# The last pass of an edge convolution: the halves of a row sum added on POOL, and one row product for each quad where there were two

## The chip, the cores and the metric

The kernel runs on one NeuronCore of a Trainium2 chip. The metric is the device time of a run in microseconds. The engines are named as in the profile: PE (TensorE, matrix products), PEld (its weight loads), DVE (VectorE), ACT (ScalarE), POOL (GpSimd) and SP (SyncE, which here only issues transfers). Each engine works through its own instructions in a fixed order and waits on semaphores where an operand comes from another engine.

## The reference

A graph with 6,250 nodes of 128 features and 200,000 edges, sorted by destination, passes through two networks: five attention layers, and then one edge convolution. The change lies in the convolution:

```python
x_src, x_dst = h[src], h[dst]
e = (x_dst - x_src) @ theta_w.T + x_src @ phi_w.T
e = relu(bn(e, bn0_g, bn0_b))      # batch norm over all edges
e = e @ fc1_w.T
e = relu(bn(e, bn1_g, bn1_b))      # batch norm over all edges
agg = segment_sum(e, dst, num_segments=n)
x = agg / maximum(cnt, 1)[:, None]
out = x0 + relu(x + h)             # h is the layer-normed x0, x0 the input plus the attention's output
```

The two batch norms need the mean and the variance over all edges before the next step can be done, so the convolution takes three passes over the edges. The last one computes the second activation and sums the edges of each destination.

## The kernel before

**Rows and quads.** The edges of a destination are put into slots of four (K = 4), padded where they don't fill the last slot. 128 slots, one on each partition, make a *quad* of 512 edges. QM = 412 quads are always worked on; more exist only for inputs that need them, under a branch on a count (`over`), and are not run here. In the convolution a *block* is GQ = 4 quads, G = 16 columns of 128 edges, so each of the three passes has 103 blocks.

**The three passes.** The first (lines 941 to 967) gathers the two nodes' terms of each edge with indirect transfers that POOL issues, and writes the pre-activations `e0_d` to DRAM. The second (1005 to 1014) reads them back, applies the first batch norm and ReLU and takes the statistics of the product with fc1. The third (1061 to 1089), the one that is changed, reads `e0_d` again and does this for each block `i`:

- SP issues the loads of `es` (1 MB, line 1065, three buffers) and of `neq` (line 1067, three buffers), a mask that says which slots belong to which destination.
- ACT applies the first batch norm and ReLU to `es` (1068), and makes the selection matrix `oh` = 1 - `neq` in float32 (1070, two buffers).
- For each quad PE multiplies four columns of 128 edges by `fs`, the scaled fc1 weights (1075), into one PSUM tile `rps` of four buffers, and DVE adds the shift `shr` on the way into `rt` (1076, two buffers).
- ACT applies the ReLU to the whole of `rt` (1077). `rt` is now, for each of four quads, four rows of 128 features on each partition, one for each edge of the slot.
- DVE adds the first two of the four to the last two (1079), giving `r2` (two buffers), with two rows per slot.
- PE adds up slots of one destination: `oh` times each of the two rows, accumulated in PSUM in `po` (1083; the profile calls it `pos`). That is two products for each quad, eight in a block.
- DVE makes the running state (1086): `state` x `keep` + `po`. `keep` is 0 where a new window of destinations begins. Each of the four updates needs the one before it. `st` has three buffers of four states.
- POOL copies each state to its place in `A2`, a table in SBUF (1089). The place is read from a register, and a later quad of the same window overwrites an earlier one.

**What sets the order.** No order is written out by hand. Tiles and their buffers are declared, and a scheduler in the framework orders the instructions of each engine when the program is built, from its own estimate of the durations, and puts in the semaphore waits. Work of neighbouring blocks is thus interleaved: in the timeline the state updates of one block stand between the additions 1076 of the next. On the chip each engine keeps that order.

After the last block, DVE and POOL combine the even and odd windows of `A2` (1096 to 1098), and DVE does the closing arithmetic (1106 to 1114).

Of the kernel before, what the change touches and what calls it, by code (L numbers as in the profile page):

```python
# [9 lines left out]
F32 = mybir.dt.float32  # L10
# [3 lines left out]
OP = mybir.AluOpType  # L14
# [7 lines left out]
P = 128  # L22
K = 4
G = 16
GQ = G // K
# [9 lines left out]
def gnn_kernel(ctx: ExitStack, tc: tile.TileContext, x, src, dst, ea, Ws, Wes, a_srcs, a_dsts, a_edges,  # L35
# [13 lines left out]
    nc = tc.nc  # L49
# [84 lines left out]
    def regs(row, q0, n, engine, top):  # L134
        _, r = nc.values_load_multi_w_load_instructions(
            tbi[32 * row:32 * row + 1, ds(q0, n)], engines=[engine], min_val=0, max_val=top, skip_runtime_bounds_check_because="blocks' views are below W2")
        return r

    def over(step, do, before=None, between=None):

        for q0 in range(0, QM, step):
            do(q0, min(step, QM - q0))
        if QM < Q:
            if between:
                between()
            n = nc.values_load_multi_w_load_instructions(more, min_val=0, max_val=P * Q, skip_runtime_bounds_check_because="a count of rows")[1][0]
            with tc.If(n > 0):
                if before:
                    before()
                for q0 in range(QM, Q, step):  # L150
                    do(q0, min(step, Q - q0))

    def mid_bc(a, n, w):
        return a[:, None, :].to_broadcast([P, n, w])

    def last_bc(a, n, w):
        return a[:, :, None].to_broadcast([P, n, w])
# [25 lines left out]
    with tc.tile_pool(name="gat", bufs=1) as gp:  # L183
# [305 lines left out]
        def rows(sp, sw, pp, then):  # L489
# [83 lines left out]
            def with_then(q0, n):  # L573
                some(q0, n)
                if q0 == 4 * RQ:
                    then()
# [203 lines left out]
        def edges(l):  # L780
            with tc.tile_pool(name="edg", bufs=2) as ep, tc.tile_pool(name="edgp", bufs=1, space=PSUM) as pp:
# [92 lines left out]
                def fixed():  # L874
                    nc.vector.tensor_copy(was, state[0])
                    state[0] = was

                over(AQ, some, lambda: nc.scalar.dma_start(ael[:, K * QM:], ae_d[l, :, K * QM:]), fixed)

        with tc.tile_pool(name="row", bufs=1) as sp, tc.tile_pool(name="roww", bufs=3) as sw, \  # L880
# [19 lines left out]
    with tc.tile_pool(name="ec", bufs=1) as gp:  # L900
# [10 lines left out]
        with tc.tile_pool(name="p1", bufs=2) as ep, tc.tile_pool(name="p1p", bufs=4, space=PSUM) as pp:  # L911
# [29 lines left out]
            def some(q0, n):  # L941
# [25 lines left out]
                nc.sync.dma_start(e0_d[c0 // G], xs.rearrange("p a b -> p (a b)"))  # L967

            over(GQ, some)

        nc.vector.tensor_reduce(S1, st0[:, 0, :], AX.X, OP.add)
# [81 lines left out]
        with tc.tile_pool(name="p4", bufs=3) as ep, tc.tile_pool(name="p4p", bufs=4, space=PSUM) as pp:  # L1053
            A2 = ep.tile([P, W2, D], F32, name="A2", bufs=1)
            A2f = A2.rearrange("p b d -> p (b d)")
            nc.gpsimd.memset(A2, 0.0)
            was = ep.tile([P, D], F32, name="was4", bufs=1)
            nc.vector.memset(was, 0.0)
            state = [was]

            def some(q0, n):
                i = q0 // GQ
                r = regs(2, q0, GQ, POOL, (W2 - 2) * P)
                es = ep.tile([P, G, P], F32, name="e4")
                nc.sync.dma_start(es.rearrange("p a b -> p (a b)"), e0_d[i])
                neq = ep.tile([P, GQ, P], BF, name="neq4")
                nc.sync.dma_start(neq, neq_d[i])
                nc.scalar.activation(es, es, AF.Relu, bias=SH0, scale=SC0)
                oh = ep.tile([P, GQ, P], F32, name="oh4", bufs=2)
                nc.scalar.activation(oh, neq, AF.Identity, bias=onec, scale=-1.0)  # L1070
                rt = ep.tile([P, GQ, K, P], F32, name="rt", bufs=2)
                for q in range(GQ):
                    ps = pp.tile([P, K, P], F32, name="rps")
                    for k in range(K):
                        nc.tensor.matmul(ps[:, k, :], es[:, K * q + k, :], fs, start=True, stop=True)
                    nc.vector.tensor_tensor(rt[:, q], ps, mid_bc(shr, K, P), OP.add)
                nc.scalar.activation(rt, rt, AF.Relu)
                r2 = ep.tile([P, GQ, K // 2, P], F32, name="r2", bufs=2)
                nc.vector.tensor_tensor(r2, rt[:, :, :K // 2, :], rt[:, :, K // 2:, :], OP.add)
                po = pp.tile([P, GQ, P], F32, name="pos")  # L1080
                for q in range(GQ):
                    for k in range(K // 2):
                        nc.tensor.matmul(po[:, q, :], oh[:, q, :], r2[:, q, k, :], start=(k == 0), stop=(k == K // 2 - 1))
                st = ep.tile([P, GQ, P], F32, name="st4")
                for q in range(GQ):
                    nc.vector.scalar_tensor_tensor(st[:, q, :], state[0], keep[:, q0 + q:q0 + q + 1], po[:, q, :], op0=OP.mult, op1=OP.add)  # L1086
                    state[0] = st[:, q, :]
                for q in range(GQ):
                    nc.gpsimd.tensor_copy(A2f[:, ds(r[q], 2 * P)].rearrange("p (a d) -> p a d", a=2), mid_bc(st[:, q, :], 2, P))  # L1089

            def fixed():
                nc.vector.tensor_copy(was, state[0])
                state[0] = was

            over(GQ, some, between=fixed)
            nc.vector.tensor_tensor(A, A2[:, 0:2 * NB:2], last_bc(mX, NB, D), OP.mult)
            nc.gpsimd.tensor_tensor(A2[:, 1:2 * NB:2], A2[:, 1:2 * NB:2], last_bc(mY, NB, D), OP.mult)
            nc.vector.tensor_tensor(A, A, A2[:, 1:2 * NB:2], OP.add)  # L1098
# [60 lines left out]
```

## Time and profile before

| | us |
|---|---|
| median of 3 runs | 17,761.48 (17,751.63 to 17,762.48) |
| profiled execution | 15,354.99 |
| its span, first to last instruction | 15,353.2 |
| last pass within it | 14,707 to 15,280 |
| closing arithmetic | 15,280 to 15,353 |

The profiled execution is one run of the same program with the hardware profiler on. It is 2,406 us shorter than the median of the runs without it; nothing in the profile says where. Times of instructions and waits come from this execution.

In the profile, `r<-rt` is the addition at 1079, with the buffer numbers left out (`r2`), `pos` is the PSUM tile `po`, `e` is the tile `es`, and `A` is `A2` in this stage. One float32 product shows as two records of 128 columns on PE, so the eight products of line 1083 in a block are 16 records. A bracket at the end of a line of a timeline is the idle time before it, with what ended it; "issue" means that the profile shows no releaser. A merged line with "x2" gives the time from the first start to the last end. Consecutive instructions of an engine overlap by some tens of nanoseconds, so distances between starts are shorter than durations.

### The profile page before, as it was taken

What the parts mean: (1) busy time and instruction counts of PE and PEld (TensorE: products, weight loads), DVE (VectorE), ACT (ScalarE), POOL (GpSimd) and SP (SyncE); (2) the same over time, 40 slices, a digit from 0 to 9 for tenths busy, and PEclk for the clock granted to TensorE, in tenths of its full rate; (3) what the DMA queues carried; (4) which work ended last, traced back from release to release, by engine and by line L of the source; (5) the groups of instructions that cost most, each with busy time, mean ns of one, the idle gap of its engine ahead of it and who ended that gap; (6) DMA issues with size and microseconds to landing.
All of it is one profiled execution on the core that took longest, in us unless ns stands there. A gap on an engine that the chain in (4) does not pass through costs nothing. (4 is left out here: it accounts for less than half of the span.)

```text
span 15353.2 us, 84839 instructions
## 1 busy us (share of the span) xinstructions
PE 3563.2 (23%) x18550; PEld 2269.4 (15%) x18550; DVE 9106.1 (59%) x14785; ACT 3161.7 (21%) x6154; POOL 10194.1 (66%) x10906
## 2 busy tenths in 40 slices
PE   5211111121111121111121111211111232222797
PEld 4100000010000010000010000100000111111377
DVE  8535666656666656666656666656666643333688
ACT  1221111111111111111111111111111211111476
POOL 1667777747777747777657777477777477777134
PEclk7555555555555555555555555555555555555899
DMA  3212222222222222222222222222222333333665
GB/s 123 61 50 71 67 67 67 66 64 67 66 67 67 64 62 67 67 67 67 60 66 67 67 67 67 57 70 67 67 67 66 91 117 111 111 113 112 230 231 192
DMA packets 722984, 1301.20 MB, mean 85 GB/s; under 512 B 207200, under 2 KB 503552, under 8 KB 682624
## 3 DMA queue, kind: packets, MB, share of 16 engines
q0 software_dynamic: 329600, 663.87, 17.7%
q1 hardware_dynamic: 356416, 587.30, 11.5%
q10 hardware_dynamic: 36416, 44.22, 0.9%
q8 instruction: 159, 2.61, 0.1%
q14 instruction: 393, 3.22, 0.1%
HBM read 1094.17 MB, written 200.45 MB: 84 GB/s over the span
## 5 line engine op out<-in xcount | busy, mean ns | idle before, releaser
L791 POOL DMA_INDIRECT g<-table,srci x8240 | 7780.3, 944 | 2565.9 <-issue 2490.9
L810 PE MATMUL xp<-ident,z 128*128 128x128 f32 x2060 | 507.2, 427 | 7548.2 <-DVE z L807 7548.2
L804 DVE TENSOR_TENSOR mt<-g,ael 128x32 f32<-128x32 f32 (+1 forms) x260 | 57.1, 219 | 3563.2 <-DMA g<-table,srci 3532.1
L945 POOL DMA_INDIRECT g<-btable,srci x1648 | 1573.0, 954 | 502.7 <-issue 478.8
L854 DVE TENSOR_REDUCE ys<-pr 128x1032 f32<-128x4128 f32 (+1 forms) x260 | 1841.4, 7082 | 8.8
L810 PEld LDWEIGHTS xp<-ident,z 128*128 128x128 f32 x2060 | 403.6, 223 | 7728.6 <-DVE z L807 7326.7
L866 PE MATMUL op<-y,oh 128*128 128x387 bf16 x2060 | 840.2, 511 | 1528.5 <-DVE ys L867 848.1
L850 DVE TENSOR_TENSOR pr<-g,mt 128x4128 f32<-128x4128 f32 (+1 forms) x260 | 1147.2, 4412 | 70.5 <-ACT mt L847 70.5
L872 ACT COPY sv<-st 128x260 f32 x2060 | 834.6, 405 | 1272.5 <-DVE u L821 1118.4
L867 DVE TENSOR_REDUCE ys<-op 128x258 f32<-128x774 f32 x1030 | 998.8, 970 | 105.7 <-PE op L866 81.9
L858 ACT CAST y<-ys 128x1032 bf16<-128x1032 f32 (+1 forms) x260 | 265.1, 1020 | 3825.7 <-DVE ys L857 3825.7
L960 DVE TENSOR_TENSOR xe<-g,ar 128x512 f32<-128x512 f32 x412 | 282.0, 687 | 1115.5 <-DMA g<-btable,srci 1115.3
L856 ACT CAST y<-ys 128x1032 bf16<-128x1032 f32 (+1 forms) x260 | 264.5, 1017 | 2816.7 <-DVE ys L854 2816.7
L516 POOL DMA_INDIRECT rg<-rec_d,rowi x412 | 468.1, 1136 | 419.6 <-ACT neqw L533 273.6
L963 PE MATMUL xps<-ident,xe 128*128 128x128 f32 x1648 | 441.7, 424 | 1239.4 <-DVE xe L960 1239.4
L869 DVE SCALAR_TENSOR_TENSOR st<-st,cor,ys 128x129 f32<-128x129 f32 x2055 | 710.6, 346 | 9.4
L966 ACT ACTIVATE sq<-xps,negc 128x512 f32<-128x512 f32 x412 | 281.6, 686 | 1699.1 <-DVE xs L964 1698.4
L963 PEld LDWEIGHTS xps<-ident,xe 128*128 128x128 f32 x1648 | 294.2, 216 | 1418.3 <-issue 1405.0
L866 PEld LDWEIGHTS <-oh 128*128 128x128 bf16 x2060 | 200.0, 119 | 1937.7 <-issue 850.3
L813 DVE TENSOR_REDUCE tm<-xp 128x8 f32<-128x1024 f32 (+1 forms) x260 | 315.7, 1214 | 238.2 <-PE xp L810 238.2
L1089 POOL COPY A<-st 128x256 f32 x412 | 248.5, 603 | 313.2 <-DVE st L1086 297.2
L861 ACT ACTIVATE oh<-neq,onesq 128x1024 bf16<-128x1024 bf16 (+1 forms) x260 | 296.1, 1139 | 475.3 <-PE op L866 428.7
(389 smaller groups left out, 9385.0 us busy)
## 6 DMA issues: line engine op xcount, KB each, us to landing
g<-table,srci POOLq DMA_INDIRECT x8240, 2.5
e_d<-xs SPq DMA_DIRECT2D x103, 1024.0 KB, 4.3
x<-e_d SPq DMA_DIRECT2D x103, 1024.0 KB, 4.8
e<-e_d SPq DMA_DIRECT2D x103, 1024.0 KB, 4.9
neq<-neq_d SPq DMA_DIRECT2D x255, 256.0 KB, 3.1
eqt<-eqt_d SPq DMA_DIRECT2D x255, 256.0 KB, 2.7
g<-btable,srci POOLq DMA_INDIRECT x1648, 2.5
table<-hb SPq DMA_DIRECT2D x80, 195.0 KB, 2.5
```

The source lines that it names most:

```text
L516: nc.gpsimd.indirect_dma_start(out=rg[:, j, :, :].rearrange("p k r -> p (k r)"), out_offset=None, in_=rec_d, in_offset=bass.IndirectOffset ...
L791: nc.gpsimd.indirect_dma_start(out=g[:, j, :], out_offset=None, in_=table, in_offset=bass.IndirectOffsetOnAxis(ap=srci[:, c0 + j:c0 + j + ...
L810: nc.tensor.transpose(xp[:, j, :], z[:, j, :], ident)
L813: nc.vector.tensor_reduce(tm[:, :n], xp[:, :n], AX.X, OP.max)
L850: nc.vector.tensor_tensor(pr.rearrange("p q k d -> p (q k) d")[:, :w], g[:, :w, :D + 1], last_bc(ex, w, D + 1), OP.mult)
L854: nc.vector.tensor_reduce(y, pr[:, :n].rearrange("p q k d -> p q d k"), AX.X, OP.add)
L866: nc.tensor.matmul(op[:, j, :3 * (D + 1)], oh[:, h + j, :], y3[:, h + j], start=True, stop=True)
L867: nc.vector.tensor_reduce(sm, op[:, :, :3 * (D + 1)].rearrange("p b (a d) -> p b d a", a=3), AX.X, OP.add)
L869: nc.vector.scalar_tensor_tensor(st[:, j, :D + 1], state[0][:, :D + 1], cor[:, j:j + 1], sm[:, j - h, :], op0=OP.mult, op1=OP.add)
L872: nc.scalar.copy(svf[:, ds(r[j], 2 * HW)].rearrange("p (a w) -> p a w", a=2), mid_bc(st[:, j, :], 2, HW))
L945: nc.gpsimd.indirect_dma_start(out=g[:, j, :], out_offset=None, in_=btable, in_offset=bass.IndirectOffsetOnAxis(ap=srci[:, c0 + j:c0 + j + ...
L963: nc.tensor.transpose(ps[:, k, :], xe[:, k, :], ident)
```

## The change

POOL adds the two rows of `r2` to one row `r1`, and PE multiplies `oh` with that one row. A block has one POOL instruction of 128 x 512 elements more and four row products instead of eight. All else stays as written: the loads, the ACT instructions, the additions and updates on DVE, and the copies on POOL. `r1` has two buffers of 2 KB on each partition.

```diff
                 r2 = ep.tile([P, GQ, K // 2, P], F32, name="r2", bufs=2)
                 nc.vector.tensor_tensor(r2, rt[:, :, :K // 2, :], rt[:, :, K // 2:, :], OP.add)
+                r1 = ep.tile([P, GQ, P], F32, name="r1", bufs=2)
+                nc.gpsimd.tensor_tensor(r1, r2[:, :, 0, :], r2[:, :, 1, :], OP.add)
                 po = pp.tile([P, GQ, P], F32, name="pos")
                 for q in range(GQ):
-                    for k in range(K // 2):
-                        nc.tensor.matmul(po[:, q, :], oh[:, q, :], r2[:, q, k, :], start=(k == 0), stop=(k == K // 2 - 1))
+                    nc.tensor.matmul(po[:, q, :], oh[:, q, :], r1[:, q, :], start=True, stop=True)
                 st = ep.tile([P, GQ, P], F32, name="st4")
```

## The prediction

> **What bounds the kernel now.** I read the stretches of the profiled span first, to find the stage that the diff touches. The last pass runs from 14,707 to 15,280 us of the 15,353.2 us span. The groups by shape give the durations, the waits in the steady part of the stage say what each engine lacks, and the timeline of each engine shows the order. The chain that ended last is of no use: it covers only the closing vector work after this stage.
>
> Columns: length, busy time and count of each engine, then PE clock, DMA share and GB/s.
> ```profile
> core 0: us, PE busy (x) PEld busy (x) DVE busy (x) ACT busy (x) POOL busy (x), PEclk, DMA share, GB/s
> 14720.00:15270.00 550.00, 548.61 (x4896) 547.40 (x4895) 483.98 (x916) 464.26 (x303) 244.16 (x404) 1.00 0.63 216
> ```
> PE has no idle time in this stage and has its full clock, so it sets the pace; DVE is busy 88%, ACT 84%, POOL 44%. The first state update begins at 14,729.1 us and the last at 15,278.6 us, 411 updates apart and four to a block: 549.5/411 x 4 = 5.348 us a block, for 103 blocks. Each engine's share of that is PE 5.35, DVE 483.98/550 x 5.348 = 4.71, ACT 4.51 us.
>
> Groups of instructions by shape (count | total, mean ns | idle before, releaser):
> ```profile
> L1075 PE MATMUL rps<-fs,e 128*128 128x128 f32 x3296 | 387.7, 276 | 4.4 <-DMA e<-e_d 4.4
> L1076 DVE TENSOR_TENSOR rt<-rps,shr 128x512 f32<-128x512 f32 x412 | 269.1, 682 | 14.5 <-PE rps L1075 9.4
> L1089 POOL COPY A<-st 128x256 f32 x412 | 248.5, 603 | 313.2 <-DVE st L1086 297.2 <-POOL A L1089 0.2
> L1083 PE MATMUL pos<-r,oh 128*128 128x128 f32 x1648 | 203.2, 277 | 4.2 <-DVE r L1079 4.2
> L1077 ACT ACTIVATE rt<-rt 128x2048 f32<-128x2048 f32 x103 | 196.7, 1909 | 30.4 <-DVE rt L1076 29.3
> L1086 DVE SCALAR_TENSOR_TENSOR st<-st,keep,pos 128x128 f32<-128x128 f32 x411 | 140.4, 342 | 62.2 <-issue 53.8 <-PE pos L1083 6.3
> L1079 DVE TENSOR_TENSOR r<-rt 128x1024 f32<-128x1024 f32 x103 | 125.4, 1217 | 1.7 <-ACT rt L1077 1.7
> ```
> A block holds 32 records of L1075 and 16 of L1083 (each float32 product is two records). Their 276 ns overlap; the pace is 5.348/48 = 111 ns.
>
> Two blocks on DVE, and what PE and POOL do meanwhile (start, duration, engine, line):
> ```profile
> 15004.19 1.22 DVE L1079 TENSOR_TENSOR r<-rt 128x1024 f32<-128x1024 f32 x1
> 15005.33 0.34 DVE L1086 SCALAR_TENSOR_TENSOR st<-st,keep,pos 128x128 f32<-128x128 f32 x1
> 15005.58 1.28 DVE L1076 TENSOR_TENSOR rt<-rps,shr 128x512 f32<-128x512 f32 x2
> 15007.63 0.35 DVE L1086 SCALAR_TENSOR_TENSOR st<-st,keep,pos 128x128 f32<-128x128 f32 x1 [0.77 <-issue]
> ...
> 15009.61 1.22 DVE L1079 TENSOR_TENSOR r<-rt 128x1024 f32<-128x1024 f32 x1
> 15010.74 0.34 DVE L1086 SCALAR_TENSOR_TENSOR st<-st,keep,pos 128x128 f32<-128x128 f32 x1
> 15011.00 1.88 DVE L1076 TENSOR_TENSOR rt<-rps,shr 128x512 f32<-128x512 f32 x3
> 15013.21 0.73 DVE L1086 SCALAR_TENSOR_TENSOR st<-st,keep,pos 128x128 f32<-128x128 f32 x2 [0.34 <-issue]
> ```
> ```profile
> 15005.58 1.95 PE L1083 MATMUL pos<-r,oh 128*128 128x128 f32 x16
> ```
> ```profile
> 15004.41 1.80 POOL L1089 COPY A<-st 128x256 f32 x2 [0.57 <-DVE st L1086]
> 15008.11 0.40 POOL L1089 COPY A<-st 128x256 f32 x1 [1.91 <-DVE st L1086]
> ```
> The reader is to see a ring. r2 ends at 15,005.41; the row product starts 0.17 later and holds PE for 1.79 us; the first state update follows 0.26 after it. That is 2.22 us from r2's end to the update. DVE fills it with the previous block's last update (0.26) and two or three additions L1076 (0.60 each: three take 1.88, of which one is 0.68), then waits 0.77 or 0.34 us. The order on each engine was fixed when the program was built, and it isn't the order of the source.
>
> **What the Trainium skill says.** "SBUF — State Buffer", section "Who interferes with whom": a DVE instruction with two SBUF inputs and a GpSimd instruction that reads SBUF lock each other out for a whole instruction. The trace agrees: a copy L1089 takes 403 ns by its median, but the two at 15,004.41 take 1.80 us; the first had to wait for r2, the one DVE operation here with two SBUF inputs. "GPSIMD Engine Reference", section 3.1, has a float32 add of 2048 elements at 4497 ns; in proportion my estimate for 512 is 1.12 us. The trace has the same shape of addition in an earlier stage, and it also shows the lock from the other side (DVE 1.69 us where 0.68 is usual):
> ```profile
> 12110.33 1.26 POOL L709 TENSOR_TENSOR xb<-xb,bb 128x512 f32<-128x512 f32 x1 [13.09 <-DVE x1c L632]
> 12110.45 1.69 DVE L716 TENSOR_TENSOR h2c<-x1c,m 128x512 f32<-128x512 f32 x1
> ```
> I take 1.26 us for the new addition; the bounds are 1.12 (the page) and 2.25 (1.26 and a full r2 in front).
>
> **The change part by part.**
> *Removed:* 8 of the 48 PE records of a block, 8 x 0.111 = 0.89 us. PE falls to 4.46 us, under DVE's 4.71. PE's whole 0.89 x 103 = 92 us can't be gained, because DVE takes over at 4.71: at most (5.348 - 4.71) x 103 = 66 us.
> *Added:* 103 additions on POOL of 1.26 us. POOL then has 2.37 (now) + 1.26 = 3.6 us of work a block, so it isn't the bound. Queued behind the addition on POOL are the copies L1089; nobody waits for those inside the stage except the state tile's third buffer, three blocks later. Its cover lost, a late copy costs nothing until it is that late. No DMA is added or moved, and SP's queue is unchanged. ACT and DVE keep their instructions. r2's buffer comes free at POOL's read instead of PE's, earlier or equal. oh is freed by the row product, which is later by the new step; oh's next write on ACT comes at 15,008.77, 1.2 us after the product ended, which just covers that.
> *Lengthened:* the ring. From r2's end: the copy that r2 locked out runs first (0.40, and 0.05), addition 1.26, hand-over to PE 0.17, product 0.89, hand-over to DVE 0.26: 3.03 us. If no copy is in front: 0.13 (the hand-over from an update to a copy, 15,004.28 to 15,004.41) + 1.26 + 0.17 + 1.15 = 2.71. So 2.71 to 3.03 against 2.22 now.
> *What hides it:* additions L1076 that DVE can do before the update. PE, not held by the row product, goes on with the next block's products while POOL adds, and PSUM holds four of them, so four additions can be there. With the update of 0.26 in front these are 0.26 + 4 x 0.60 = 2.66 us: DVE waits 0.05 to 0.37, mean 0.21. The other waits of DVE in this stretch were for products and for ACT, 6.6 us, 0.06 a block. Sum: 4.71 + 0.21 + 0.06 = 4.98 us a block. DVE is the bound then, so every further wait costs its full length. If the cover is gone altogether, with two additions as at 15,005.58, the wait is 1.25 to 1.57.
>
> Gain: (5.348 - 4.98) x 103 = 38 us. The profiled execution's 15,354.99 us (span 15,353.2 and 1.8 us around it) would be about 15,317. The median of the runs shown is 17,761.48, which is 2,406 us above the profiled one; the profile can't show where. I take this stage to be the same in both and subtract there: 17,723. If everything were stretched alike (1.157), it would be 44 us.
>
> **The rivals.** They differ in how many additions the fixed order leaves between r2 and the first update.
> *A, four:* as above, -38 us (own range -65, no waiting, to -20). For it: PE is free for 1.6 us more before the row product. 48 in 100.
> *A', more than DVE's limit:* if PE's clock without the profiler is below the 1.00 shown, PE stays the bound and all of its saving counts: at 0.9 of the clock 0.89/0.9 x 103 = -102 us. Nothing speaks for it but the 2,406 us. 6 in 100.
> *B, three or a mixture of three and four:* work 2.06 to 2.36, waits 0.35 to 0.97, period 5.12 to 5.74; the means of the two ends give -7 us for the mixture and +24 for three. The removed PE time has turned into DVE waits. 20 in 100, 4 of them beyond the bound.
> *C, slower, the order stays as it is:* two and three in turn, mean work 1.76, waits 0.95 to 1.27, period 5.72 to 6.04: +38 to +71, mean +55 us, 17,816. It decides from a wait of 0.92 us a block on, where the period passes 5.69. For it: DVE's additions there are now just those that were ready before the row product, and the order's maker may price the POOL step too low and the lock not at all. Against it: that maker placed PE's products with no idle time now. 26 in 100.
> *DMA takes over:* 1 MB a block lands in 4.9 us, share 0.63; at 4.98 us the share is 0.68, and the stage before this one ran at 0.83 (14,500 to 14,600 us). Excluded as the bound.
>
> **How the numbers follow.** 0.2% is 35.5 us, about what a measurement of this kernel tells from no change. Faster beyond it: 42 of A's 48 and A', 48 in 100. Within: 6 of A and 16 of B, 22. Slower: C and 4 of B, 30. Time of the likeliest: 17,723, its own range 17,696 to 17,741. The range over the cases, A to most of C: 17,690 to 17,822.
>
> **What would show it.** Right: L1083 with 824 records, PE at about 0.9 busy in this stage, DVE at 0.94 or more, the POOL addition at 1.2 to 1.8 us, four L1076 between r2 and the first update, and its wait under 0.4 us. C: two or three there and waits near 1 us, PE with idle time before L1083 put down to POOL. Wrong in size: a DVE r2 longer than 1.22 (locked out by POOL), an addition behind several copies, ACT waiting at L1070 for the product, or a PE clock under 1.00 in the gaps.

## The result, and the profile after

| | before | after |
|---|---|---|
| median, us | 17,755.09 | 17,816.7 |
| runs | 7 (17,751.63 to 17,770.11) | 7 (17,803.64 to 17,824.07) |
| ratio, 95% interval | | 1.0033 [1.0023, 1.0042] |
| last pass, first to last state update, us | 549.5 | 610.6 |
| the same for a block (411 updates, four to a block) | 5.348 | 5.943 |

The kernel became slower by 62 us (17,816.7 - 17,755.09). The stage alone grew by 610.6 - 549.5 = 61.1 us, so the difference lies in the last pass. Outside it, the order of the instructions is the same on every engine. The profiled run after took 17,815.91 us (span 17,814.0), the one before 15,354.99; the two fell on chips that differ in the earlier stages, which is taken up at the end. In everything that follows, medians are compared with runs of the kernel before on the same chip, and the stage by its own length.

The stretch of the last pass in the kernel after, in the columns of the same view of before:

```profile
core 0: us, PE busy (x) PEld busy (x) DVE busy (x) ACT busy (x) POOL busy (x), PEclk, DMA share, GB/s
17155.00:17705.00 550.00, 443.00 (x3691) 425.28 (x3689) 430.25 (x830) 418.40 (x277) 317.18 (x461) 0.99 0.59 199
```

Before, PE was busy for 548.61 of 550 us. Now no engine is: PE is busy 81%, DVE 78%, ACT 76%, POOL 58%. Each of the four has idle time, so none of them sets the pace by its own work alone, and a chain through several of them has to be looked for. What each engine lacks stands in the groups by shape (count | total us, mean ns | idle before, by releaser). The lines have moved: the product is 1084, the update 1087, the copies 1090.

```profile
L1076 DVE TENSOR_TENSOR rt<-rps,shr 128x512 f32<-128x512 f32 x412 | 274.9, 682 | 8.9 <-PE rps L1075 8.8
L1087 DVE SCALAR_TENSOR_TENSOR st<-st,keep,pos 128x128 f32<-128x128 f32 x411 | 139.6, 340 | 120.2 <-PE pos L1084 81.7 <-POOL A L1090 25.3 <-issue 13.0
L1081 POOL TENSOR_TENSOR r<-r 128x512 f32<-128x512 f32 x103 | 130.7, 1269 | 46.5 <-DVE r L1079 46.2 <-PE rps L1075 0.2 <-DVE st L1087 0.2
L1079 DVE TENSOR_TENSOR r<-rt 128x1024 f32<-128x1024 f32 x103 | 125.6, 1219 | 16.1 <-POOL A L1090 14.7 <-ACT rt L1077 1.4
L1084 PE MATMUL pos<-r,oh 128*128 128x128 f32 x824 | 124.7, 297 | 123.6 <-POOL r L1081 123.6
```

The row product has half of its records, 824. The idle time before it is 123.6 us, 1.20 us a block, all put down to the new addition. DVE's idle time before the state updates has doubled from 62.2 to 120.2 us, 1.17 us a block. The new addition itself takes 1,269 ns. The last column of r2's row needs care: the profile puts 14.7 of its 16.1 us down to a copy on POOL, but in each of the 26 waits r2 starts 0.10 us after the end of the ReLU on ACT, so it is the ReLU that was late. The longest waits of PE, ACT and DVE in the steady part (engine, line, what it waited for: us in total, times, longest):

```profile
PE pos L1084 <- POOL r L1081: 106.7, 91, 2.1
ACT oh L1070 <- issue: 92.0, 40, 2.9
DVE st L1087 <- PE pos L1084: 72.5, 69, 1.2
```

One block of the kernel after, on DVE, POOL and PE in turn (start, duration, engine, line; idle time before in brackets):

```profile
17512.69 1.22 DVE L1079 TENSOR_TENSOR r<-rt 128x1024 f32<-128x1024 f32 x1
17513.82 1.88 DVE L1076 TENSOR_TENSOR rt<-rps,shr 128x512 f32<-128x512 f32 x3
17516.73 0.35 DVE L1087 SCALAR_TENSOR_TENSOR st<-st,keep,pos 128x128 f32<-128x128 f32 x1 [1.02 <-PE pos L1084]
```
```profile
17512.90 1.27 POOL L1090 COPY A<-st 128x256 f32 x1 [0.45 <-DVE st L1087]
17514.13 1.27 POOL L1081 TENSOR_TENSOR r<-r 128x512 f32<-128x512 f32 x1
```
```profile
17515.46 1.16 PE L1084 MATMUL pos<-r,oh 128*128 128x128 f32 x8 [0.42 <-POOL r L1081]
```

r2 ends at 17,513.91. It had held up a copy on POOL, which takes 1.27 us where it would take 0.40, so the addition starts 0.22 us after r2's end (0.15 in the block before, where no copy is in front) and ends at 17,515.40. The row product follows at 17,515.46 and takes 1.00 us to the next product's start, then the update comes at 17,516.73: 2.82 us from r2's end, where it was 2.22. DVE has three additions to do in this time and waits 1.02 us. In the other three blocks of a cycle of four, the order on DVE leaves two additions between r2 and the first update, with one or two updates of the block before. That work is 1.80, 1.72, 1.72 and 1.46 us, 1.67 on the mean, against the 2.82 that pass until the update can start.

### The profile page after: what moved, and what is told of

Same layout as the page of the kernel before. It is cut to its first block, busy times and chain, and to the rows that moved or that the text cites. A ratio compares the mean times of both kernels' runs of the same rounds, so it can differ in the third digit from the quotient of the medians.

```text
span 17814.0 us, 83593 instructions
## 1 busy us (share of the span) xinstructions
PE 3445.5 (19%) x17726; PEld 2206.1 (12%) x17726; DVE 9086.1 (51%) x14785; ACT 3175.6 (18%) x6154; POOL 10316.7 (58%) x11009
## 5 line engine op out<-in xcount | busy, mean ns | idle before, releaser
L842 DVE TENSOR_REDUCE am<-mt 128x16 f32<-128x48 f32 (+1 forms) x260 | 53.8, 207 | 3514.6 <-remote 3405.4
L964 DVE TENSOR_SCALAR_CACHE_REDUCE xs<-xps,negc 128x512 f32<-128x512 f32 x412 | 308.3, 750 | 1499.1 <-remote 1135.8
L856 ACT CAST y<-ys 128x1032 bf16<-128x1032 f32 (+1 forms) x260 | 264.6, 1018 | 2785.5 <-DVE ys L854 1909.9
L963 PE MATMUL xps<-ident,xe 128*128 128x128 f32 x1648 | 380.2, 409 | 1513.6 <-DVE xe L960 1440.7
L1075 PE MATMUL rps<-fs,e 128*128 128x128 f32 x3296 | 391.2, 278 | 4.4 <-ACT e L1068 4.4
L1075 PEld LDWEIGHTS rps<-fs,e 128*128 128x128 f32 x3296 | 383.1, 195 | 4.7 <-ACT e L1068 4.7
```

The source lines that it names most:

```text
L963: nc.tensor.transpose(ps[:, k, :], xe[:, k, :], ident)
```

## The experiments

Two theories stood against each other at first. The *ring*: r2, addition on POOL, row product, update, the DVE work in the fixed order, next r2 goes round once a block and is now longer than everything else. The *selection matrix*: ACT waits 92 us at `oh` for buffers that the later row product frees late, so the ReLU, and with it r2, come late. Other candidates were the lock between DVE and POOL of which the prediction speaks, and PE's clock in its new gaps. The stage lengths of all runs, before 549.5 and after 610.6 us:

| kernel | stage, us | a block, us | median, us | before, same chip | ratio [95%] |
|---|---|---|---|---|---|
| after with three `oh` | 605.0 | 5.888 | 17,894.07 | 17,833.47 | 1.0030 [1.0019, 1.0042] |
| half of the sum left out | 468.1 | 4.556 | 17,751.9 | 17,833.47 | 0.9952 [0.9936, 0.9969] |
| addition on DVE | 560.1 | 5.451 | 17,846.82 | 17,833.47 | 1.0008 [0.9999, 1.0017] |
| before with the addition unread | 549.3 | 5.346 | 17,831.9 | 17,833.47 | 0.9998 [0.9989, 1.0007] |
| after, sums a block behind | 559.2 | 5.442 | 17,836.58 | 17,823.19 | 1.0006 [0.9997, 1.0015] |
| before, sums a block behind | 565.2 | 5.501 | 17,840.53 | 17,823.19 | 1.0009 [1.0000, 1.0018] |
| two POOL instructions | 695.3 | 6.767 | 17,971.89 | 17,823.19 | 1.0084 [1.0067, 1.0101] |
| after, behind, five `oh` | 556.9 | 5.420 | 17,777.57 | 17,770.71 | 1.0002 [0.9994, 1.0011] |
| before, behind, five `oh` | 566.8 | 5.516 | 17,784.06 | 17,770.71 | 1.0009 [1.0003, 1.0016] |
| after, behind, `oh` tied | 504.8 | 4.913 | 17,762.17 | 17,802.16 | 0.9975 [0.9964, 0.9985] |
| after, `oh` tied alone | 609.4 | 5.931 | 17,860.44 | 17,802.16 | 1.0031 [1.0021, 1.0041] |
| before, behind, `oh` tied | 571.4 | 5.561 | 15,391.36 | 15,367.36 | 1.0016 [1.0009, 1.0023] |

### Is it the selection matrix's buffers?

```diff
-                oh = ep.tile([P, GQ, P], F32, name="oh4", bufs=2)
+                oh = ep.tile([P, GQ, P], F32, name="oh4", bufs=3)
```

> The changed kernel with three buffers for the selection matrix oh where it has two; the order on every engine stays that of the changed kernel. Two rings are in question. Ring A: r2, POOL's addition, the row product, the state update, with too few additions of DVE in between. Ring B: the row product frees oh, ACT writes the next oh and has the ReLU of the next block queued behind that wait, and r2 needs this ReLU. If ring A sets the pace, ACT's wait of 107 us at L1070 goes and a block still takes 5.8 to 5.95 us (17,800 to 17,817 us). If ring B does, a block falls to 5.4 us or less, and the run to 17,765 us or less. The port lock (POOL's addition behind a copy that r2 held up) expects what ring A expects.

The stage took 605.0 us, 5.6 less than after and 55.5 more than before. But the edit didn't take away what it was meant to. Waits of this kernel, from 17,200 to 17,700 us:

```profile
ACT oh L1070 <- PE pos L1084: 48.4, 24, 2.5
ACT oh L1070 <- issue: 41.3, 20, 2.2
```

The run was expected to take this wait away, and it didn't: ACT still waits 89.7 us at `oh`. With a third buffer the scheduler put the instruction one block earlier in ACT's order, where it waits for a product all the same. So this run doesn't tell the theories apart. The next one ties `oh`: it holds it behind the ReLU of its own block.

```diff
-                oh = ep.tile([P, GQ, P], F32, name="oh4", bufs=2)
-                nc.scalar.activation(oh, neq, AF.Identity, bias=onec, scale=-1.0)
...
-                nc.scalar.activation(rt, rt, AF.Relu)
+                ri = nc.scalar.activation(rt, rt, AF.Relu)
+                with tc.issue_after(ri.ins):
+                    oh = ep.tile([P, GQ, P], F32, name="oh4", bufs=4)
+                    nc.scalar.activation(oh, neq, AF.Identity, bias=onec, scale=-1.0)
```

> The changed kernel with only the making of oh tied behind the ReLU (four buffers); the updates stay where the scheduler puts them. In this order a block has three updates, two additions and r2 between its first update and the end of the next r2: 0.77 + 1.20 + 1.14 = 3.11 us. The first ring alone then gives 3.11 + 2.8 = 5.9 us a block, 50 to 65 us over the kernel before, as the changed kernel. If the ring through oh and the ReLU was the cause, 5.4 us or less.

Now neither `oh` nor r2 waits at all:

```profile
L1080 DVE TENSOR_TENSOR r<-rt 128x1024 f32<-128x1024 f32 x103 | 125.4, 1217 | 0.0
L1078 ACT ACTIVATE oh<-neq,onesq 128x512 f32<-128x512 bf16 x103 | 72.8, 707 | 0.0
```

The stage is 609.4 us, as long as after's, so the whole slowdown is there without the selection matrix. The two kernels differ in one more thing: the tie also changed the order on DVE, and every block now has two additions and one update between r2 and its own first update, 1.46 us where after has 1.67 on the mean. That is 0.21 us a block, 22 us in all, which r2's lost wait of 16.1 us and a clock that doesn't fall (3 to 4 us, see the end) about made up for. In after itself the late ReLU can therefore have a part; r2's idle time there is 16.1 us of the 61. In the tied kernel the ring stands alone. DVE, from one r2 to the next, and PE's row product in it:

```profile
17406.41 1.22 DVE L1080 TENSOR_TENSOR r<-rt 128x1024 f32<-128x1024 f32 x1
17407.55 0.34 DVE L1088 SCALAR_TENSOR_TENSOR st<-st,keep,pos 128x128 f32<-128x128 f32 x1
17407.81 1.28 DVE L1074 TENSOR_TENSOR rt<-rps,shr 128x512 f32<-128x512 f32 x2
17410.43 0.35 DVE L1088 SCALAR_TENSOR_TENSOR st<-st,keep,pos 128x128 f32<-128x128 f32 x1 [1.34 <-POOL A L1091]
...
17412.41 1.22 DVE L1080 TENSOR_TENSOR r<-rt 128x1024 f32<-128x1024 f32 x1
```
```profile
17409.18 1.16 PE L1085 MATMUL pos<-r,oh 128*128 128x128 f32 x8 [1.26 <-POOL r L1082]
```

The profile names a copy as what ended the 1.34 us. That copy had ended at 17,409.47; the update starts 0.26 us after the row product's 0.99 us (9.18 to the next product's start at 10.17), so it was the product that released it. From update to next r2 DVE has 1.98 us of work (three updates of 0.26 and two additions of 0.60), r2 takes 1.22, and from r2's end at 17,407.63 to the update 2.80 pass. 1.98 + 1.22 + 2.80 = 6.00, the distance of the two r2 (the mean over the stage is 5.931). PE's clock is 1.00 throughout the steady part of this kernel, so the clock isn't needed for the slowdown either.

### What would the fewer products be worth without the ring?

The addition is taken out, and the product takes the first row of r2 alone. This leaves half of each row's sum out of the result.

```diff
-                r1 = ep.tile([P, GQ, P], F32, name="r1", bufs=2)
-                nc.gpsimd.tensor_tensor(r1, r2[:, :, 0, :], r2[:, :, 1, :], OP.add)
...
-                    nc.tensor.matmul(po[:, q, :], oh[:, q, :], r1[:, q, :], start=True, stop=True)
+                    nc.tensor.matmul(po[:, q, :], oh[:, q, :], r2[:, q, 0, :], start=True, stop=True)
```

> The changed kernel without POOL's addition: the row product takes the first row of r2 alone, so half of each row's sum is left out. PE has the same 40 records a block as the changed kernel. It prices what the removal of the products alone is worth. From r2's end to the first update there are 0.17 + 0.89 + 0.26 = 1.32 us, less than DVE's 1.46 of work between them in the order, so that ring is no limit: a block at DVE's 4.71 to 4.95 us, 41 to 66 us under the kernel before (17,690 to 17,715). If instead ACT or the loads are the limit at this pace, 5.1 us or more.

468.1 us, 81.4 less than before; the medians differ by 81.6. The stretch in the steady part:

```profile
17230.00:17640.00 410.00, 410.00 (x3600) 408.24 (x3599) 409.96 (x809) 404.57 (x270) 221.40 (x360) 1.00 0.77 261
```

The 4.56 us a block are under the 4.71 to 4.95 that were expected. DVE is never idle here: four additions of 0.60, one r2 of 1.14 to the next start, four updates of 0.255, together 4.56. PE shows no idle time either, and its eight row records take 0.99 us here and not 0.89; with 32 records at 0.111 that is 4.54, so it is close to its own limit. The loads aren't the limit in any of the slower kernels, as they keep up with this pace, at a DMA share of 0.77. The prediction's DVE bound of 4.71 was too high. It came from the busy share of a stretch in which DVE waits about twice a block. Consecutive instructions overlap, so the last one before a wait counts some 0.08 us more than it takes in a row of work (an update 0.34 for 0.26, an addition 0.68 for 0.60). So 81 us lay in the fewer products, if nothing stood in the ring in their place.

### The addition on another engine, and beside the ring

The addition goes to DVE:

```diff
-                nc.gpsimd.tensor_tensor(r1, r2[:, :, 0, :], r2[:, :, 1, :], OP.add)
+                nc.vector.tensor_tensor(r1, r2[:, :, 0, :], r2[:, :, 1, :], OP.add)
```

> The changed kernel with its addition on DVE where it is on POOL. No hand-over to POOL, no lock and no queueing behind copies, but DVE gets 512 elements more: 0.60 us by L1076, so 4.71 + 0.60 = 5.31 us a block. If only POOL's latency made the change slow, a block takes 5.3 to 5.45 us, the run 17,750 to 17,766 us, as before. If the order of the changed kernel (oh ahead of the ReLU on ACT) is what costs, it stays at 5.7 us or more.

560.1 us, 5.451 a block. The addition takes 682 ns on DVE by its row, about half of POOL's. It then stands in DVE's own work, 4.556 + 0.60 = 5.16 us a block; the other 0.29 weren't reckoned through. PE's idle time before the row product is 67.7 us where after has 123.6. ACT waits 84.5 us at `oh` here too, so these waits alone don't make a block as long as after's. It is 50 us better than after and 11 us longer in the stage than before; by the medians it isn't told from before.

The other way round, the kernel before is left as it is, with its eight products, and POOL does the addition into a tile that nobody reads:

```diff
                 nc.vector.tensor_tensor(r2, rt[:, :, :K // 2, :], rt[:, :, K // 2:, :], OP.add)
+                r1 = ep.tile([P, GQ, P], F32, name="r1", bufs=2)
+                nc.gpsimd.tensor_tensor(r1, r2[:, :, 0, :], r2[:, :, 1, :], OP.add)
```

> The kernel before with POOL's addition put beside it: r1 is computed and nothing reads it; PE has its eight products of r2 as before, and the order on PE, DVE and ACT is that of before. It prices the port lock and POOL's load alone. If the lock or POOL's queue is the cause, r2 gets longer than 1.22 us or the copies hold something up, and a block takes over 5.5 us. If a ring is the cause, nothing changes: 5.33 to 5.38 us a block, within 10 us of the kernel before.

549.3 us against 549.5, and the median is before's on the same chip, ratio 0.9998 [0.9989, 1.0007]. POOL's work, its lock with DVE (r2's mean is 1,221 ns, before 1,217) and r2's buffer held by POOL cost nothing. It is the addition's place in the ring that costs, and not that it is done. This stage of 549.3 us belongs to a run of over 17,800 us; before's 549.5 to one of 15,355. With the medians alike, so are the stages, and the last pass is the same on both kinds of chip.

### Making the ring longer

```diff
                 nc.gpsimd.tensor_tensor(r1, r2[:, :, 0, :], r2[:, :, 1, :], OP.add)
+                nc.gpsimd.tensor_tensor(r1, r1, mid_bc(onesq, GQ, P), OP.mult)
```

> The changed kernel with POOL's step doubled: after the addition POOL multiplies r1 by ones, another 1.26 us in front of the row product. In the order of this program each block has, from its first update to the end of the next r2, two updates, one addition and r2: 0.26 + 0.60 + 0.26 + 1.14 = 2.26 us. If the ring sets the pace, a block takes this and r2's end to update, 2.8 + 1.27 = 4.1: 6.3 to 6.6 us, 98 to 130 us over the kernel before. If POOL's latency is not in the ring, 5.9 to 6.0 us as in the changed kernel.

The second instruction, a product by one, takes 1,278 ns. The stage grew to 695.3 us, 6.767 a block, somewhat more than the 6.3 to 6.6 expected. r2 never waits here, though ACT waits 161 us at `oh`: in this kernel the selection matrix holds nothing up.

```profile
L1079 DVE TENSOR_TENSOR r<-rt 128x1024 f32<-128x1024 f32 x103 | 125.6, 1219 | 0.0
L1070 ACT ACTIVATE oh<-neq,onesq 128x512 f32<-128x512 bf16 x103 | 74.4, 722 | 161.0 <-PE pos L1085 158.8 <-issue 2.1
```
```profile
17403.92 1.22 DVE L1079 TENSOR_TENSOR r<-rt 128x1024 f32<-128x1024 f32 x1
17409.51 0.35 DVE L1088 SCALAR_TENSOR_TENSOR st<-st,keep,pos 128x128 f32<-128x128 f32 x1 [2.06 <-POOL A L1091]
17410.63 1.22 DVE L1079 TENSOR_TENSOR r<-rt 128x1024 f32<-128x1024 f32 x1
```

The trace has the sum of it: 6.71 us pass from one r2 to the next (17,403.92 to 17,410.63), of which r2 takes 1.22, the way from its end to the update 4.37 and the way from there to the next r2 1.12. In the tied kernel above these were 1.22, 2.80 and 1.98. So the ring's middle became longer by 1.57 us, 1.22 for the instruction and 0.35 for a copy that stands between the two on POOL, and the order made up for 0.86 of it by moving two DVE instructions (an addition and an update) ahead of the wait: 6.00 + 1.57 - 0.86 = 6.71. Eleven blocks take up to 0.92 us more, as the next one with 7.63: there PE's clock falls in the gap, and the eight records take 1.87 us for 0.99. POOL, DVE, ACT and PE all have idle time in this kernel; the period follows the ring.

### Cutting the ring

The row product, the updates and the copies of a block, unchanged, go into a function `back` that is called one block later, tied behind the r2 of the next block on the engines' orders. Now a block's addition has the time of a whole block before its product is wanted:

```diff
-                nc.vector.tensor_tensor(r2, rt[:, :, :K // 2, :], rt[:, :, K // 2:, :], OP.add)
+                r2i = nc.vector.tensor_tensor(r2, rt[:, :, :K // 2, :], rt[:, :, K // 2:, :], OP.add)
...
+                def back():
...
+                if pend:
+                    with tc.issue_after(r2i.ins):
+                        pend.pop()()
+                pend.append(back)
```

With three `oh` buffers, once on the kernel after and once, as a control, on the kernel before:

> The changed kernel with the row product, the updates and the copies of a block written one block later, and the updates tied behind the next block's r2 on DVE (oh has three buffers for it). DVE then has a whole block of its own work between an r2 and the update that needs it. If the ring r2, POOL's addition (2.8 us to the update), update, next r2 made the change slow, it is open now and DVE's own work is the limit, 4.56 us a block as in the run with one row: 4.56 to 4.80 us, a stage of 468 to 493 us, 56 to 81 us under the kernel before. If POOL's addition costs by itself (lock, load), 5.3 us or more remain.

> The kernel before with the same later writing and the same tie, and its eight products a block; POOL adds nothing. It tells whether the order alone gives the gain. PE has 48 records a block and was never idle: 5.33 to 5.40 us a block, within 10 us of the kernel before. If the order of before had itself cost time, a gain of over 20 us.

After's stage fell from 610.6 to 559.2 us, and it was 605.0 with three `oh` buffers alone, so cutting the ring took away 46 to 51 us; it is then 6 us shorter than the control's 565.2. Both missed what was expected: 468 to 493 us for the first, and for the control a stage within 10 us of before, where it is 16 longer. The updates on DVE wait 2.5 us in all, where it was 120.2. But the fewer products' 81 us aren't there: PE still has 81.3 us of idle time before the row product, r2 now waits 60.9 us, 53.2 of them for the ReLU, and ACT 77.2 us at `oh`:

```profile
L1080 DVE TENSOR_TENSOR r<-rt 128x1024 f32<-128x1024 f32 x103 | 137.3, 1333 | 60.9 <-ACT rt L1078 53.2 <-ACTq L147 1.1
L1086 PE MATMUL pos<-r,oh 128*128 128x128 f32 x824 | 120.2, 289 | 81.3 <-POOL r L1082 81.1
L1071 ACT ACTIVATE oh<-neq,onesq 128x512 f32<-128x512 bf16 x103 | 73.5, 714 | 77.2 <-issue 67.8 <-PE pos L1086 9.4
```

A second ring has come up behind the first: row product, free `oh` buffer, `oh`, ReLU, r2, addition, row product. The next pair has five buffers for `oh`:

> The changed kernel with the later, tied updates, and now five buffers for oh where the run before had three. That run took 5.443 us a block; ACT waited 64 us in 440 for the row product at the instruction that makes oh, with the ReLU behind it, and DVE 46 us for the ReLU. If this second ring (product, oh, ReLU, r2, addition, product) is what was left, ACT's wait at oh is gone and a block takes 4.6 to 4.9 us, a stage of 473 to 504 us, 45 to 76 us under the kernel before. If the loads or ACT's own work are what is left, 5.2 us or more.

> The kernel before, eight products a block and no addition on POOL, with the later, tied updates and five buffers for oh: the control for the run above. If a gain there comes from the fewer products, this one is bound by PE at 5.33 to 5.40 us a block, within 10 us of the kernel before. If order and buffers alone are worth it, over 30 us faster.

The edit beside the one above is the number of buffers:

```diff
-                oh = ep.tile([P, GQ, P], F32, name="oh4", bufs=3)
+                oh = ep.tile([P, GQ, P], F32, name="oh4", bufs=5)
```

556.9 and 566.8 us: 2 us less and 2 us more than with three, where 473 to 504 us were expected of the first, and of the second again a stage within 10 us of before. ACT of the kernel after with five buffers shows why:

```profile
17407.73 0.71 ACT L1071 ACTIVATE oh<-neq,onesq 128x512 f32<-128x512 bf16 x1
17409.16 0.72 ACT L1071 ACTIVATE oh<-neq,onesq 128x512 f32<-128x512 bf16 x1 [0.73 <-PE pos L1086]
17409.79 1.89 ACT L1078 ACTIVATE rt<-rt 128x2048 f32<-128x2048 f32 x1
```

As with three buffers in the first experiment, the scheduler used the room to put `oh` further ahead. The second one waits 0.73 us for a row product to free a buffer, and the ReLU stands behind it. More buffers moved the wait to another block and left it. So the order has to be held instead, with the tie of `oh` behind the ReLU that was shown above, in one kernel with the sums a block behind:

> The changed kernel with the later, tied updates, and now the making of oh tied behind the ReLU of its own block on ACT (four buffers). More buffers alone left ACT waiting 54 us in 470 at oh for the row product, because the scheduler only makes oh that much earlier, ahead of the ReLU. If this second ring was what was left (5.42 us a block), the waits at oh and DVE's waits for the ReLU (43 us) go and a block takes 4.6 to 4.9 us: a stage of 473 to 504 us, 45 to 76 us under the kernel before. If PE's waits for POOL's addition (63 us) set the pace instead, 5.2 us or more.

504.8 us, 4.913 a block, at the end of the 473 to 504 expected: 105.8 us less than after and 44.7 less than before. The median is 40 us under before's, ratio 0.9975 [0.9964, 0.9985]. It beats both kernels. Groups of it:

```profile
L1081 DVE TENSOR_TENSOR r<-rt 128x1024 f32<-128x1024 f32 x103 | 136.3, 1324 | 11.6 <-ACT rt L1076 5.3
L1079 ACT ACTIVATE oh<-neq,onesq 128x512 f32<-128x512 bf16 x103 | 72.8, 706 | 0.0
L1090 DVE SCALAR_TENSOR_TENSOR st<-st,keep,pos 128x128 f32<-128x128 f32 x411 | 137.7, 335 | 2.5 <-PE pos L1087 2.2
```

`oh` doesn't wait, and the updates hardly. Of the 4.913 us, 4.556 are DVE's own work. r2 takes 1.21 us in one block and 1.47 in the next, where a copy on POOL holds it up, and then starts 0.22 us late as well: (0.26 + 0.22)/2 = 0.24 us a block. In every second block an addition starts 0.23 us late, which is the last 0.11; what it waits for the profile doesn't name. That the gain comes from the fewer products and not from the ties is the control's part, the same ties on the kernel before:

> The control for the run at 4.913 us a block: the kernel before, eight products a block and no addition on POOL, with the same later, tied updates and oh tied behind the ReLU. If that run's gain comes from the four products fewer, this one is bound by PE's 48 records: 5.33 to 5.40 us a block, within 10 us of the kernel before. If the ties alone are worth it, 5.2 us or less.

571.4 us, 22 more than before without the ties, where at most 10 were expected, and 67 more than the same ties with the fewer products. PE is busy all the time in it, as in before, but its stream has a break once a block. Its weight loads for the row product, before and here:

```profile
L1083 PEld LDWEIGHTS pos<-r,oh 128*128 128x128 f32 x1648 | 193.6, 193 | 5.6 <-DVE r L1079 5.3
L1086 PEld LDWEIGHTS pos<-r,oh 128*128 128x128 f32 x1648 | 193.1, 193 | 20.4 <-issue 17.3 <-ACTq L147 3.1
```

In before PE's records start 0.11 us apart nearly all through. Here the first two of each row product start 0.27 and 0.18 us after the one ahead of them: 0.23 us more a block, 24 us in 103 blocks, about the difference. The two controls above have the same break with 0.17 us, and they are 16 and 17 us longer than before. What makes the break isn't shown. So the eight products are dearer under the ties than in before, and of the 67 us between the tied pair, about 22 are this break.

## Why the prediction was wrong

The prediction, 17,723 us, fell on the other side. Case C, at 26 in 100, is what happened: two and three additions between r2 and the first update, DVE waits near 1 us, PE idle before the row product and put down to POOL. It gave +38 to +71 us with a mean of +55; measured are +62 by the medians and +61 in the stage. Point by point:

- **Four additions can be there: this step failed.** The prediction let PE run on with the next block's products while POOL adds, and took for granted that DVE's order would use them. PE didn't run on: it stood idle before the row product, 1.20 us a block. And the order on DVE leaves three, two, two and two additions. The work between r2 and the update is 1.67 us on the mean where 2.66 were wanted. The order did react: on PE the row product stood behind three or four of the sixteen column products of the block after next, and now stands behind eight or twelve. That is still too early for it, by 1.23, 0.42, 1.29 and 1.83 us in the four blocks of a cycle. An order that is fixed when the program is built doesn't shift by itself when a product comes late: PE waits with the column products behind it, and DVE waits at the update with the other additions behind it; at an addition it has no wait in the steady part. What price the scheduler set for the POOL addition isn't shown; that it set it too low is only argued.
- **The length of the ring, 2.71 to 3.03 us: right as a sum.** 2.82 in after, 2.80 in the tied kernel, a held-up copy in front in both. Its parts are off in both directions: in the block shown the copy costs 0.22 and not 0.45, the hand-over to PE 0.06 and not 0.17, and the product 1.00 and not 0.89. That they cancel is in part luck.
- **The addition, 1.26 us: right.** 1,269 ns. "SBUF — State Buffer", section "Who interferes with whom", in the Trainium skill has DVE with two SBUF inputs and GpSimd lock each other out; a copy of 1.27 us beside r2 agrees. By itself the lock costs nothing in this stage, 549.3 us against 549.5; it counts only where the instruction that is held up lies in a ring.
- **PE's part, eight records fewer: right in count,** 824. Its 0.89 us weren't the gain, as the prediction said. That PE would have idle time and lose its clock in it was named as a sign only and had no price.
- **DVE takes over at 4.71: mis-sized.** It is 4.556, and the most that could be gained 81 us, not 66. By this sum, case A with its four additions would have been better than forecast.
- **oh's next write "just covers": mis-sized.** ACT waits 92 us there in the steady part, with 1.2 us of cover beforehand. In after r2's wait for the late ReLU, 16.1 us, is what comes of it; where the first ring is cut it costs 54 us (504.8 against 559.2).
- **Period of case C, 5.72 to 6.04 us: right,** 5.943, and in part by luck. In the four blocks of a cycle the way from the first update to the end of the next r2 takes 2.34, 2.34, 3.28 and 4.05 us without waits, 3.00 on the mean, and 2.81 for the way back to an update make 5.81. r2's wait for the late ReLU adds 0.16 (16.1/103): 5.97, which is the mean of the stage without its first and last five blocks. The forecast lacked this 0.16 and took 1.76 us of cover where 1.67 are there, but its DVE term was 0.15 too high.

Case C was on the list, and its reckoning held; the weight went to A. The trace of before showed two and three additions in turn, and what the prediction held against their staying so was how PE's products are placed, not how the order on DVE would change.

## What to carry to other kernels

Moving a step off the busiest engine doesn't take it out of the chain that goes round once a block: add up that chain beside each engine's sum, and count as cover only work that the present order shows in that place. Of an added instruction ask whether a later step of that chain waits for it: 1.27 us a block on POOL cost nothing where nobody read the result, and turned 81 us of gain into 61 us of loss where the row product did. Where a scheduler sets the order, another buffer may only let it issue the waiting instruction earlier; writing the consumer one block later and tying the order of both took the waits away (610.6 to 504.8 us).

## What the runs showed of the hardware

PE's clock fell to half after short gaps. Stretches of the kernel after around one of them:

```profile
17506.00:17507.70 1.70, 0.00 (x0) 0.00 (x0) 1.70 (x4) 0.97 (x1) 1.24 (x2) 1.00 0.95 400
17507.70:17509.00 1.30, 1.22 (x6) 1.22 (x7) 0.06 (x1) 0.00 (x0) 0.37 (x2) 0.58 0.48 183
17509.00:17510.00 1.00, 1.00 (x7) 1.00 (x7) 0.14 (x1) 0.15 (x1) 0.00 (x0) 0.50 0.02 8
```

The gap is 1.84 us, and the clock goes to 0.50 soon after the row product starts; its eight records then take 1.77 us where they take 0.99 in most blocks, and the clock is back some 3.5 us after the product's start. It happened after five of the 24 waits of 1.83 to 1.84 us, and in the kernel with two POOL instructions after 11 of the 88 waits of 1.71 to 1.73. In the tied kernel, where PE waits about 1.26 us in every block, it never happened. "TensorE: Matmul & The Clock Gate", section "What's actually happening", in the Trainium skill puts the fall at an idle window of about 3.4 us that runs on its own clock; here gaps of about half of that were enough at times. At some 0.8 us each, the row products of the stage lost 3 to 4 us by it, so PE's clock isn't what made the kernel slower by 61.

Chips differ in earlier stages. One chip runs the kernel before in 15,367 us, others in 17,755 to 17,833, with the same order of instructions: the attention stage's last product of line 840 starts at 12,060 us in the profile of before and at 14,146 in that of after, 2,086 us later. Most of the rest of the 2,406 us that the prediction couldn't place comes in the convolution's first pass. Both stages gather rows with indirect transfers that POOL issues, and what they wait for differs, before and after:

```profile
L791 POOL DMA_INDIRECT g<-table,srci x8240 | 7780.3, 944 | 2565.9 <-issue 2490.9 <-DVE was L783 57.0 <-DMA g<-table,srci 18.0
L791 POOL DMA_INDIRECT g<-table,srci x8240 | 7791.4, 946 | 4584.1 <-issue 2471.0 <-DVE pr L850 2054.0 <-DVE was L783 57.0
```

By the profile, on the slower chip POOL waits 2,054 us for DVE in the attention stage, and 321 us in the first pass (line 945), against nothing and 2 us. The last pass isn't touched by it, as 549.3 and 549.5 us show. Why POOL waits there on one chip and not on the other stays open.
